# Two attention layers on one core: the output projection by the twice-applied seven-product scheme, in one row with k and q

## The chip, the cores and the metric

The kernel runs on one core of a Trainium2 chip. The metric is device time in microseconds, the median of several executions. A core has a matrix engine (TensorE, PE in the profile, with its weight loads as PEld), a vector engine (DVE), a scalar engine (ACT), a general engine (GpSimd, POOL) that is hardly used here, and a sync engine (SP) that issues all transfers of this kernel. Each takes its instructions in the order in which they were written; they wait for each other with semaphores. Products collect in PSUM, everything else on chip lies in SBUF, and weights and images come from and go to device memory (HBM).

## What is computed

Two attention layers follow each other on an input of 8 images with 512 channels and 32 x 32 = 1024 tokens, all in 32-bit floats. One layer is:

```
xn = group_norm(x) * gamma + beta            # 8 groups of 64 channels
q, k, v = Wq xn + bq, Wk xn + bk, Wv xn + bv # each 512 x 512 times 512 x 1024
e = exp(q^T k / 8)                           # 8 heads of 64 channels, 1024 x 1024 each
o = (e v) / (row sums of e)
x = x + Wp o + bp
```

## The kernel before

**Jobs.** An image in a layer is a job. The 16 jobs go in the order image 0 and 1 in layer 0, the same in layer 1, then images 2 and 3, and so on (`jobs`). Between the attention of job n and that of job n+1 lies a boundary; there are 15. At a boundary stand, on TensorE, the v product of job n+1 (`v_phase`), the output product of job n (`proj_phase`), and then k and q of job n+1 (`deep_phases`). After the last job a plain product stands instead (`plain_proj`).

**Seven products.** A product of two matrices cut into 2 x 2 blocks can be made with seven block products in place of eight, at the price of sums: some of blocks before (of weights, `factor`, kept in HBM by `store_factors`; of activations, `combine` and `inner_sums`), some of products after. `chain` does the sums after on four PSUM banks, named z, y, u and w by their use. Products 1, 6, 7 and 4 collect in z one after the other; between them z is copied (to y after 1, to u after 6) or read out (by `put(1, 1, z)` after 7 and `put(1, 0, z)` after 4). Product 3 collects in u. Product 4 can therefore not write z before `put(1, 1, z)` has read it. In `put` the results of the left half of the tokens go by the scalar engine, those of the right half by the vector engine. v and the output use the scheme once; both go in steps of half a block product, with the banks of one half of PSUM for each step in turn (`half_phase`). k and q use it twice: an outer scheme of seven products (order `OUTER`: 1, 2, 6, 5, 7, 3, 4), each of which is a chain of seven matmuls of 128 x 128 by 256 (order `ORDER`: 1, 5, 6, 2, 7, 3, 4). The chains overlap: position 7c + 2j orders product j of chain c. After products 7 and 3 of a chain one waiting addition of the outer scheme (`outer`) is issued, or an extra piece of work if there is none.

**Attention.** 64 steps per job (`Attention.run`): step i makes the scores of a block (four quarter matmuls of 512), their exponential on the scalar engine into one of five tiles e, the addition of that tile to `acc` on the vector engine (`add`), and the product of an earlier tile with v (`values`, two steps behind). Every eighth step ends a group (`finish`): DVE reduces `acc` to row sums r and joins the two halves of po into q's place (which then holds o); after every second group the sums r go through lr (by DMA), are inverted into rt (`invert`), written out to rd and read back as rb, repeated over 64 rows; `normalise` multiplies. Other work is put between the steps as `chores` with a step number: the group norm of the next job (`groups`, then `scale` and `shift`) and the sums of its blocks (`sums`).

**Order.** For TensorE, ACT and DVE the order is the order in which Python issues; a virtual clock (`advance`, `later`) decides when delayed pieces are issued, and knows nothing of an engine's load. Weights come through a ring of eight tiles (`fetch`, `plan`), a new one when an old one is used up. Tiles of one name take the same place: to with k, the block sums `deep` with raw weights that jobs 0 to 2 factor during attention, `acc`, `px` and `rb` with two places each, and x with two.

**Where the change touches.** `half_phase` from line 401, `v_phase`, `proj_phase` from line 455 (L469 the output products, L476 and L481 its results on DVE), `deep_phases` from line 492 (L538 the products, L552 and L554 results on DVE, L570 the outer additions), `combine` (L332 to L338), `inner_sums` (L370 to L376), `out_sums`, `deep_sums`, `make_out_bias`, and the main loop. Unchanged, but spoken of: L659 scores, L664 exponentials, L674 and L676 additions to `acc`, L690 values, L703 and L710 the end of a group, L724 to L730 the inversion, L740 the normalisation.

Of the kernel before, what the change touches and what calls it, by code (L numbers as in the profile page):

```python
# [70 lines left out]
def fast_path(  # L71
# [21 lines left out]
    out_bias = acts.tile([P, 2, NC], F32, name="out_bias")  # L93
    bias_step = acts.tile([P, 2, 2, 2], F32, name="bias_step")
# [71 lines left out]
    def fetch():  # L166


        if not plan or len(held) == RING:
            return  # L170
        key = plan.popleft()
        n, which, o = key
        layer = jobs[n][1]
        w = ring.tile([P, NW, P], F32, tag="w", name=f"w_{which}_{n}_{o}")
        held[key] = w
        if which in (V, O):
            nc.sync.dma_start(wide(w), factors[which, layer][:, FACTOR[o]])
        elif (which, layer, o) in deep:
            nc.sync.dma_start(w, deep[which, layer, o])
        else:  # L180
            if o in BLOCK:
                src = raw_block(layer, which, *BLOCK[o])
            else:
                src = factors[which, layer][:, FACTOR[o]]
            nc.sync.dma_start(wide(w), src)
            raw.add(key)
# [214 lines left out]
    def half_phase(n, which, src, t, group, order):  # L401

        steps = []
        for i in range(2):
            z, y, u, w = (bank(i, b, f"{b}_{which}_{n}_{i}") for b in "zyuv")
            steps.append(chain(*group(i), z, y, u, w))
        thunks = []
        for o in order:
            key = (n, which, o)
            thunks.append(lambda o=o: (steps[0](o), advance(1.72)))  # L410

            def second(o=o, key=key):
                steps[1](o)
                if key in held:
                    used(key)
                advance(1.72)

            thunks.append(second)
        return thunks

    def v_phase(n, order, first=None):
# [31 lines left out]
        return half_phase(n, V, src, tx, group, order)  # L453

    def proj_phase(n):
        b, layer = jobs[n]
        xt, src = xs[b], qt[0]

        def group(i):
            s5 = epool.tile([P, 2, HALF], F32, tag="e", name=f"s5o_{n}_{i}")  # L460

            def at(oh, sh):
                return xt[:, 2 * oh + i, sh * HALF : (sh + 1) * HALF]

            def product(o, ps, start):
                w = wide(held[n, O, o])
                r = right(src, to[0], o)
                for cc in range(2):
                    nc.tensor.matmul(  # L469
                        ps, w[:, cc, i * P : (i + 1) * P], r[:, cc, :],  # L470
                        start=(start and cc == 0), stop=(cc == 1), skip_group_check=True,
                    )

            def put5(ps):
                for oh in range(2):
                    nc.vector.tensor_add(s5[:, oh, :], ps, at(oh, 1))  # L476

            def put(oh, sh, ps):
                oc = 2 * oh + i
                more = s5[:, oh, :] if sh == 1 else at(oh, 0)  # L480
                nc.vector.scalar_tensor_tensor(  # L481
                    at(oh, sh), ps, out_bias[:, layer, oc : oc + 1], more, ALU.add, ALU.add
                )
                if layer == 1:
                    cols = slice(sh * HALF, (sh + 1) * HALF)
                    nc.sync.dma_start(out[b, oc * P : (oc + 1) * P, cols], at(oh, sh))

            return product, put5, put

        return half_phase(n, O, src, to, group, ORDER)  # L490

    def deep_phases(n, extra=()):
# [3 lines left out]
        extra = deque(extra)  # L496
        layer = jobs[n][1]
        dst = {}
        chains = [(K, o) for o in OUTER] + [(Q, o) for o in OUTER]
        tiles = {}  # L500

        def begin(c):
            which, o = chains[c]
            if o == OUTER[0]:
# [3 lines left out]
            if c + 2 < len(chains):  # L508
                prepare((n,) + chains[c + 2])
# [3 lines left out]
            half = c % 2  # L513
# [3 lines left out]
            r = right(xn[0], tx[0], o)  # L517
            if o in (4, 5, 6):
                sums = deep_t[0][:, :, {5: 0, 6: 1, 4: 2}[o], :]
            else:  # L520
                at = {1: 0, 7: 1, 2: 2, 3: 3}[o]
                sums = deep_x[0][:, :, at, :]
            moving = {
                1: r[:, 0, :QT], 2: r[:, 1, :QT], 3: r[:, 1, QT:],
                5: sums[:, 0, :], 6: sums[:, 1, :], 7: sums[:, 2, :], 4: sums[:, 3, :],
            }
            lhs = held[n, which, o]

            def bias(oo):
                if o in (1, 6, 7):  # L530
                    return None
                if o == 3:
                    return bias_step[:, layer, int(which == Q), oo : oo + 1]
                oc = oo if o == 2 else 2 + oo
# [23 lines left out]
        def end(c):  # L558
            which, o = chains[c]
            used((n, which, o))  # L560
            d = dst[which]

            def quarter(oh, sh):
                return d[:, 2 * oh : 2 * oh + 2, sh * HALF : (sh + 1) * HALF]
# [4 lines left out]
            def add(to_, a, b):  # L569
                outer.append(lambda: nc.vector.tensor_add(to_, a, b))  # L570

# [15 lines left out]
        outer = deque()  # L587

        def thunk(c, j):
            def go():  # L590
# [3 lines left out]
                if ORDER[j] in (7, 3):  # L594
                    if outer:
# [3 lines left out]
                if j == 6:  # L599
                    end(c)  # L600
                    if c + 1 == len(chains):
                        while outer:
                            outer.popleft()()
                        while extra:
                            extra.popleft()[1]()
# [3 lines left out]

        at = sorted((7 * c + 2 * j, c, j) for c in range(len(chains)) for j in range(7))  # L610
# [173 lines left out]
    def out_sums(n, src):  # L784
        def start():
            to[0] = acts.tile([P, 3, 2, HALF], F32, tag="k", name=f"to_{n}")
            combine(src, to[0], 0)

        later(12.6, start)
        for part in range(1, 4):  # L790
            later(12.6 + part * 1.7, lambda part=part: combine(src, to[0], part))

    def deep_sums(n, direct_at, other_at):


        def start():
            d = acts.tile([P, 4, 7, QT], F32, tag="deep", name=f"deep_{n}")
            deep_x[0], deep_t[0] = d[:, :, :4, :], d[:, :, 4:, :]

        later(direct_at - 0.1, start)  # L800
        for part in range(4):
            later(direct_at + 1.7 * part, lambda part=part: inner_sums(part, True))
            later(other_at + 1.7 * part, lambda part=part: inner_sums(part, False))
# [6 lines left out]
    def make_out_bias(layer, delay):  # L810
# [3 lines left out]
            apool.tile([P, 2, HALF], F32, tag="acc", name=f"rows_{layer}_{i}") for i in range(2)  # L814
# [8 lines left out]
        def part(oc):  # L823
# [3 lines left out]
            if oc == NC - 1:  # L827
# [3 lines left out]
                )  # L831

# [3 lines left out]
    def first_factors(chores, which_layers):  # L836
# [8 lines left out]
        chores[3] = start  # L845
        at = 14
        for i, (which, layer) in enumerate(which_layers):
            for part in range(4):
                at += 4
                chores[at] = lambda i=i, part=part: factor(box[0][:, i], part)  # L850
            chores[at + 1] = lambda i=i, which=which, layer=layer: store_factors(
                box[0][:, i], layer, which
            )
# [105 lines left out]
    deep_sums(0, 0.2, 12.0)  # L959
# [5 lines left out]
    rest = first[-1:]  # L965
    for n in range(-1, len(jobs)):
        last = n + 1 == len(jobs)
        if n >= 0:
            chores = {}
            if last:  # L970
                w = plain_weights(n)
            else:
                t = sums(n + 1)
                chores = dict(zip(range(2, 18), reads)) if n == 0 else {}
                chores.update(zip((24, 36, 40, 44, 48, 52), steps))
                chores.update({56: t[0], 60: t[1]})
                more = {}
                if n == 0:
                    first_factors(more, [(O, 0), (V, 1)])
                elif n == 1:  # L980
                    first_factors(more, [(K, 1), (Q, 1)])
                elif n == 2:
                    first_factors(more, [(O, 1)])
                for i, fn in more.items():
                    while i in chores:
                        i += 1
                    chores[i] = fn
                chores[61] = lambda: (extend_plan(n + 1), [fetch() for _ in range(RING)])
# [9 lines left out]
            t[2]()  # L998
            t[3]()
            out_sums(n, qt[0])  # L1000
            deep_sums(n + 1, 4.0, 27.0)
            if n in (0, 2):
                make_out_bias(jobs[n][1], 19.0)
            for thunk in v_phase(n + 1, ORDER):
                thunk()
            proj = proj_phase(n)
            for thunk in proj[:-1]:
                thunk()
            rest = proj[-1:]
        reads = steps = []  # L1010
        if n + 2 < len(jobs):
            reads, steps = norm_steps(n + 2)
        if n < 0:
            extra = [(0, lambda part=part: factor(q0, part)) for part in range(4)]
            extra.append((1, lambda: store_factors(q0, 0, Q)))
        else:
            extra, reads = [(7, fn) for fn in reads], []
        both = deep_phases(n + 1, extra)
        prepare((n + 1, K, OUTER[0]))
        prepare((n + 1, K, OUTER[1]))  # L1020
        both[0]()
        rest[0]()
        if n >= 0 and jobs[n][1] == 1 and jobs[n][0] + 2 < B:
            x_tile(jobs[n][0] + 2)
            load_x(jobs[n][0] + 2)
# [4 lines left out]
        att_n = n + 1  # L1030
        banks(0, "two")
        att = Attention(att_n)
# [254 lines left out]
```

## Time and profile before

| | |
|---|---|
| median of 3 executions | 3257.69 us (3254.89 to 3257.72) |
| the profiled execution | 3255.77 us, its span 3254.0 us |
| PE busy | 3238.2 us |
| DVE busy | 2569.5 us |
| ACT busy | 1729.5 us |
| from one job's first v product to the next job's | 201.57 us for most jobs, 203.08 once |
| additions L674 and L676 | 896, 1.22 us each |
| output: matmuls of 512 columns (L469) | 840 records in pairs |
| block sums for k and q (L370 to L376) | 64 of 1024 (1.21 to 1.23 us) and 64 of 768 (0.95 us) |

A line of the profile's groups names a source line, engine, operation, what is written and read, shape and count; then busy time and mean duration in ns; then the idle time of the engine ahead of it and what ended it. A line of the timeline has the start from the beginning of the span, the duration, the engine and line, and in square brackets the idle time ahead of it. In windows, each row is a stretch of time with its length, then the busy time of each engine. A matmul of 32-bit floats stands as two records.

### The profile page before, as it was taken

The numbers are of one execution on the slowest core, as the hardware profiler recorded it, in microseconds if no ns is written. First come the engines' busy times: TensorE is split into PE (matmuls) and PEld (weight loads), VectorE is DVE, ScalarE is ACT, GpSimd is POOL, SyncE is SP. The second block draws the span as 40 slices with busy tenths as digits, with TensorE's granted clock in tenths as the row PEclk, the third lists the DMA queues.
The fourth block names the chain that finished last, engine by engine and source line by source line (L and its number), as shares of the span: only waits on it lengthen the run. The fifth ranks groups of instructions, "written<-read, shape, count | busy, mean of one in ns | idle before, by whom it ended". The sixth has DMA issues, their size and how long they took to land.

```text
span 3254.0 us, 55636 instructions
## 1 busy us (share of the span) xinstructions
PE 3238.2 (100%) x22240; PEld 1730.1 (53%) x22240; DVE 2569.5 (79%) x3371; ACT 1729.5 (53%) x2561; POOL 14.4 (0%) x31
## 2 busy tenths in 40 slices
PE   9999999999999999999999999999999999999999
PEld 7356473564735547355463654636556364563643
DVE  8987978879687796868968689686886868868676
ACT  4636636366463664636546365463654636546363
POOL 0000000000000000000000000000000000000000
PEclk9999999999999999999999999999999999999999
DMA  8233251320502213032150311304114031130401
GB/s 299 73 112 93 71 167 57 112 96 26 176 19 79 66 32 116 15 114 85 35 164 16 93 54 38 109 16 148 51 42 157 18 105 40 48 99 22 132 21 49
DMA packets 149082, 265.53 MB, mean 82 GB/s; under 512 B 47832, under 2 KB 59216, under 8 KB 147792
## 3 DMA queue, kind: packets, MB, share of 16 engines
q1 hardware_dynamic: 148816, 261.91, 25.9%
q8 instruction: 176, 2.88, 0.4%
q14 instruction: 90, 0.74, 0.1%
HBM read 214.84 MB, written 44.89 MB: 80 GB/s over the span
## 4 chain that ended last, share of the span: by engine, by line
PE 97%; DVE 2%; DMA 0%; issue 0%; ACT 0%; SPq 0%; POOL 0%; DVEq 0%
PE sc L659 27%; PE po L690 27%; PE vd L538 8%; PE zd L538 7%; PE z L434 7%; PE z L469 6%; PE yd L538 3%; PE ud L538 3%; PE u L434 2%; PE v L434 2%; PE y L434 2%; PE y L469 2%; PE u L469 2%; PE v L469 2%; PE pp L628 1%; DVE p L554 0%
## 5 line engine op out<-in xcount | busy, mean ns | idle before, releaser
L664 ACT ACTIVATE e<-sc 128x1024 f32<-128x1024 f32 x1024 | 1046.6, 1024 | 585.7 <-PE sc L659 495.0
L659 PE MATMUL sc<-q,k 64*64 64x512 f32 x8192 | 1061.6, 590 | 0.0
L690 PE MATMUL po<-e,v 64*64 64x512 f32 x8192 | 1057.2, 589 | 0.0
L676 DVE TENSOR_TENSOR acc<-acc,e 128x1024 f32<-128x1024 f32 x768 | 938.1, 1222 | 72.7 <-ACT e L664 17.0
L690 PEld LDWEIGHTS po<-e,v 64*64 64x64 f32 x8192 | 312.9, 133 | 566.1 <-issue 551.9
L659 PEld LDWEIGHTS sc<-q,k 64*64 64x64 f32 x8192 | 309.9, 133 | 558.8 <-issue 546.1
L538 PE MATMUL vd<-deep,w 128*128 128x256 f32 x960 | 271.1, 383 | 4.5 <-DVE p L554 3.9
L674 DVE TENSOR_TENSOR acc<-e,e 128x1024 f32<-128x1024 f32 x128 | 155.9, 1218 | 108.9 <-ACT e L664 107.1
L538 PE MATMUL zd<-deep,w 128*128 128x256 f32 x832 | 232.8, 380 | 2.8 <-DVE p L552 2.0
L538 PEld LDWEIGHTS vd<-deep,w 128*128 128x128 f32 x960 | 179.4, 190 | 48.1 <-issue 13.0
L538 PEld LDWEIGHTS zd<-deep,w 128*128 128x128 f32 x832 | 157.7, 190 | 32.4 <-issue 6.9
L703 DVE TRANSPOSE_TENSOR_REDUCE r<-acc 128x32 f32<-128x1024 f32 x128 | 158.6, 1239 | 0.6
L385 ACT COPY yd<-vd 128x256 f32<-128x256 f32 x128 | 45.7, 357 | 185.1 <-PE vd L538 178.2
L740 DVE TENSOR_TENSOR q<-q,rb 128x512 f32<-128x512 f32 x128 | 83.3, 681 | 43.0 <-DMA rb<-rd 43.0
L469 PE MATMUL z<-to,w 128*128 128x512 f32 x240 | 110.3, 592 | 0.0
L434 PE MATMUL z<-w,xn 128*128 128x256 f32 x480 | 110.1, 382 | 0.0
L434 PE MATMUL z<-w,t 128*128 128x256 f32 x480 | 108.6, 379 | 0.0
L469 PE MATMUL z<-q,w 128*128 128x512 f32 x240 | 107.9, 592 | 0.0
L434 PEld LDWEIGHTS z<-w,xn 128*128 128x128 f32 x480 | 90.0, 190 | 23.8 <-issue 12.2
L389 ACT COPY u<-z 128x512 f32<-128x512 f32 x62 | 35.3, 570 | 121.8 <-PE z L469 85.1
L434 PEld LDWEIGHTS z<-w,t 128*128 128x128 f32 x480 | 91.0, 190 | 12.6 <-DVE v L449 0.2
L447 ACT COPY v<-z 128x512 f32<-128x512 f32 x32 | 18.8, 586 | 146.4 <-PE z L434 136.1
(172 smaller groups left out, 3385.2 us busy)
## 6 DMA issues: line engine op xcount, KB each, us to landing
w<-deep SPq DMA_DIRECT2D x196, 448.0 KB
w<-keep SPq DMA_DIRECT2D x226, 256.0 KB
rb<-rd SPq DMA_DIRECT2D x256, 128.0 KB
out_dram<-x SPq DMA_DIRECT2D x64, 256.0 KB
x<-x_dram SPq DMA_DIRECT2D x28, 512.0 KB
deep<-w SPq DMA_DIRECT2D x28, 448.0 KB
keep<-raw SPq DMA_DIRECT2D x5, 1792.0 KB
lr<-r SPq DMA_DIRECT2D x256, 8.0 KB
```

The lines of the kernel that those rows point to most:

```text
L385: nc.scalar.copy(y, z)
L389: nc.scalar.copy(u, z)
L434: nc.tensor.matmul(ps[:, ti * CH : (ti + 1) * CH], r[:, cc, t0 : t0 + P], w[:, cc, :], start=(start and ti == 0 and cc == 0), stop=(cc == ...
L469: nc.tensor.matmul(ps, w[:, cc, i * P : (i + 1) * P], r[:, cc, :], start=(start and cc == 0), stop=(cc == 1), skip_group_check=True,)
L538: nc.tensor.matmul(ps, lhs[:, FACTOR[i], :], moving[i], start=start, stop=True, skip_group_check=True,)
L659: nc.tensor.matmul(sc[h * HD : (h + 1) * HD, j, :], k[r, hp, k0 : k0 + HD], q[r, hp, sh * HALF : (sh + 1) * HALF], start=True, stop=True,)
L664: nc.scalar.activation(e, sc, AF.Exp, scale=SCALE)
L674: nc.vector.tensor_add(acc[g], self.es[i - 1], e)
L676: nc.vector.tensor_add(acc[g], acc[g], e)
L690: nc.tensor.matmul(po[g][j * HD : (j + 1) * HD, h, :], v[r, kc, d0 : d0 + HD], e[r, j, :], start=(kc == 0), stop=(kc == NT - 1),)
L703: nc.vector.tensor_reduce(self.r[:, m, :], self.acc.pop(g).rearrange("p j (b e) -> p (j b) e", e=RP), AX.X, ALU.add, apply_transpose=True,)
L740: nc.vector.tensor_mul(place[i], place[i], rb[i])
```

## The change

The output product also becomes a double scheme. Its seven outer products are the first seven chains of a row of 21, with k and q behind them; `proj_phase` is gone. Each O chain needs its activations as block sums of a quarter: `OutputSums` makes them on DVE, four of 128 x 256 per chain, those of five chains in v's phase (`out_sums`) and those of the last two in the row, as `soon`. The results of a chain go to a tile p with the bias (`out_bias`, and `out_step` for outer product 3), and 11 additions of 128 x 1024 bring the p tiles into x. A finished quarter of x is written out as one transfer of 512 KB (two of 256 KB before). Weights of O are factored a second time at their first use and then kept in HBM as those of k and q are, 448 KB per outer product in place of 256.

Moved with it: the group norm of the next job stands at earlier steps of attention, all four sums for v stand in attention (two of them stood after it), and from job 3 on the eight block sums for k and q stand in attention steps 46 to 60 (they stood in v's phase and the output). In jobs 0 to 2 three of these stay near the start of v's phase and five fall at the start of the row. The bias row products move from the output's phase into v's, the load of the next x to the second chain of k, and the statistics of the next norm to q's chains, with what is left over in the next attention. The last half steps of v change places, and the row of 21 begins in the other half of PSUM.

```diff
-    def proj_phase(n):
...
+    def sums_of_four(r, slots):
+        def blk(a, b):
+            return r[:, a, b * QT : (b + 1) * QT]
+        def first():
+            nc.vector.tensor_sub(slots[0], blk(0, 1), blk(0, 0))
+            nc.vector.tensor_sub(slots[1], blk(1, 1), slots[0])
+        def second():
+            nc.vector.tensor_sub(slots[2], blk(1, 1), blk(0, 1))
+            nc.vector.tensor_sub(slots[3], blk(1, 0), slots[1])
+        return first, second
...
+    def deep_phases(n, extra, outs=None):
...
-        chains = [(K, o) for o in OUTER] + [(Q, o) for o in OUTER]
+        chains = [(which, o) for which in ((O, K, Q) if outs else (K, Q)) for o in OUTER]
...
+            if which == O and c in (3, 4):
+                soon.extend(outs.steps(c + 2))
...
-            half = c % 2
+            half = (c + len(chains)) % 2
...
+            if which == O:
+                r = right(outs.src, to[0], o)
+                sums = outs.at[c]
...
+            if which == O:
+                b, layer = jobs[m]
+                xt = xs[b]
+                def more(oh, sh, *parts):
+                    to_ = xt[:, 2 * oh : 2 * oh + 2, sh * HALF : (sh + 1) * HALF]
+                    for part in parts:
+                        add(to_, to_, p(part))
...
+                if o == 1:
+                    more(0, 0, 1)
+                elif o == 2:
+                    more(0, 0, 2)
+                    done(0, 0)
+                elif o == 6:
+                    add(p(6), p(6), p(1))
+                    more(0, 1, 6)
+                elif o == 5:
+                    more(0, 1, 5)
+                elif o == 7:
+                    add(p(7), p(7), p(6))
+                    more(1, 1, 7, 5)
+                    done(1, 1)
+                elif o == 3:
+                    more(1, 0, 7)
+                    more(0, 1, 3)
+                    done(0, 1)
+                elif o == 4:
+                    more(1, 0, 4)
+                    done(1, 0)
+                return
...
                 if ORDER[j] in (7, 3):
+                    if soon:
+                        soon.popleft()()
                     if outer:
                         outer.popleft()()
...
-    def out_sums(n, src):
+    def out_sums(n, outs):
...
+        steps = outs.steps(0) + [start] + outs.steps(1) + [part(1)] + outs.steps(2)
+        steps += outs.steps(3) + [part(2)] + outs.steps(4) + [part(3)]
+        for i, step in enumerate(steps):
+            later((10.4 if i < 2 else 11.6) + 0.8 * i, step)
...
-                t = sums(n + 1)
-                chores = dict(zip(range(2, 18), reads)) if n == 0 else {}
-                chores.update(zip((24, 36, 40, 44, 48, 52), steps))
-                chores.update({56: t[0], 60: t[1]})
...
+                for i, fn in enumerate(reads if n == 0 else [fn for _, fn in extra]):
+                    put(2 + i, fn)
+                for i, fn in zip((18, 26, 28, 30, 32, 34, 37, 40, 42, 44), steps + sums(n + 1)):
+                    put(i, fn)
+                if n > 2:
+                    for i, fn in enumerate(deep_steps(n + 1)):
+                        put(46 + 2 * i, fn)
...
-            t[2]()
-            t[3]()
-            out_sums(n, qt[0])
-            deep_sums(n + 1, 4.0, 27.0)
+            outs = OutputSums(n)
+            out_sums(n, outs)
             if n in (0, 2):
-                make_out_bias(jobs[n][1], 19.0)
-            for thunk in v_phase(n + 1, ORDER):
-                thunk()
-            proj = proj_phase(n)
-            for thunk in proj[:-1]:
-                thunk()
-            rest = proj[-1:]
+                later(0.5, lambda layer=jobs[n][1]: make_out_bias(layer, 3.5))
+            if n <= 2:
+                for i, step in enumerate(deep_steps(n + 1)):
+                    later((1.0 if i < 3 else 20.0) + 1.5 * i, step)
+            first = v_phase(n + 1, ORDER)
+            for thunk in first[:-1]:
+                thunk()
+            rest = first[-1:]
```

## The prediction

> **What bounds the kernel now.** I read the page's busy shares and chain first, then the chain in order of time, then the busy time by stage of one late period (job 10 to job 11, then job 11's attention), last the vector engine's (DVE's) timeline at one stage boundary.
>
> ```profile
> PE 3238.2 (100%) x22240; PEld 1730.1 (53%) x22240; DVE 2569.5 (79%) x3371; ACT 1729.5 (53%) x2561; POOL 14.4 (0%) x31
> PE 97%; DVE 2%; DMA 0%; issue 0%; ACT 0%; SPq 0%; POOL 0%; DVEq 0%
> ```
>
> ```profile
> 418.69 3.45 PE z L434 x16
> 422.14 3.43 PE z L469 x8
> ...
> 1003.99 3.65 PE z L434 x16
> ```
>
> TensorE never rests, so its work is the time. In the chain by time, each of V's seven products (line 434) is eight matmuls of 256 columns, two records each, in 3.45 us: 0.431 us a matmul. Each output product (line 469) is four of 512 columns in 3.43 us, 0.858 each.
>
> ```profile
> 2213.40:2237.60 24.20, 24.20 (x116) 21.33 (x113) 20.73 (x26) 5.80 (x10) 0.00 (x0) 1.00 0.33 89
> 2237.60:2261.70 24.10, 24.10 (x59) 10.87 (x59) 10.35 (x14) 3.22 (x6) 0.00 (x0) 1.00 0.62 187
> 2261.70:2303.80 42.10, 42.10 (x202) 36.17 (x204) 29.24 (x48) 26.15 (x68) 0.00 (x0) 1.00 0.54 184
> 2303.80:2415.00 111.20, 110.99 (x1027) 39.53 (x1019) 97.33 (x114) 72.93 (x76) 0.53 (x1) 1.00 0.08 21
> ```
>
> The rows are V, output, k and q, attention; after the length come PE, PEld, DVE, ACT busy. DVE has 14 us to spare in attention of 111, and 14 in the output stage of 24: it is second everywhere, and close.
>
> ```profile
> 1005.15 1.25 DVE L703 TRANSPOSE_TENSOR_REDUCE r<-acc 128x32 f32<-128x1024 f32 x1
> 1006.32 0.65 DVE L710 TENSOR_TENSOR q<-po,px 128x512 f32<-128x512 f32 x1
> ...
> 1010.13 0.59 DVE L724 TENSOR_REDUCE lt<-lr 32x64 f32<-32x256 f32 x1 [0.90 <-DMA lr<-r]
> 1010.75 0.54 DVE L725 RECIPROCAL ri<-lt 32x64 f32<-32x64 f32 x1
> 1011.33 0.29 DVE L727 STREAM_TRANSPOSE rt<-ri 32x32 f32<-32x32 f32 x2
> ...
> 1016.76 0.69 DVE L740 TENSOR_TENSOR q<-q,rb 128x512 f32<-128x512 f32 x1 [1.37 <-DMA rb<-rd]
> 1018.77 0.69 DVE L740 TENSOR_TENSOR q<-q,rb 128x512 f32<-128x512 f32 x1 [1.31 <-DMA rb<-rd]
> ...
> 1061.07 0.42 DVE L552 TENSOR_TENSOR p<-zd,s 128x256 f32<-128x256 f32 x1 [1.67 <-PE zd L538]
> 1061.41 1.22 DVE L570 TENSOR_TENSOR k<-p,p 128x1024 f32<-128x1024 f32 x1
> 1062.54 0.42 DVE L552 TENSOR_TENSOR p<-ud,s 128x256 f32<-128x256 f32 x1
> ```
>
> V of this boundary (job 4 to job 5) starts at T0 = 1003.99, the chain's last line above. The last heads' sums leave DVE at T0+2.4, return through lr 3.7 us later, go out through rd and rb, and q is complete only at T0+15.4. Starts also show what an instruction occupies: 1.13 us for 1024 elements, 0.60 for 512, 0.34 for 256 (0.40 with a bias), about 0.13 more where it reads what the instruction just ahead wrote (three accumulating adds take 3.78).
>
> [...]
>
> **The change part by part.** TensorE, output: 28 matmuls x 0.858 = 24.0 us become 49 x 0.431 = 21.1. Gain 2.9 us at each of 15 boundaries, 44 in all. The scalar engine gets the same per-chain copies as in k and q (26 us in 42) and stays hidden.
>
> DVE, output: four sums of two and eight results (4 x 0.60 + 8 x 0.66 = 7.7 us) go; 14 results of 256 (5.2), 11 adds of 1024 (12.4) and 28 block sums of 256 (about 10.2) come: 20 us more per boundary. Two sums of xn move from V into attention, and from job 3 on (12 boundaries) all eight block sums for k and q too: 4 x 1.13 + 4 x 0.87 = 8.0 us.
>
> *Attention, jobs 3 to 14.* A running sum over DVE's instructions in the order of the changed program, from the add of e37, which starts 43.9 us ahead of T0: 24 adds 27.1, nine dependent gaps 1.2, four reductions 4.6, four q<-po 2.4, four normalisations 2.4, one inversion 1.9, four sums of xn 4.5, eight block sums 8.0. That is 52.1 us of work in 43.9, so q<-po ends at T0+8.3. The same sum over the order of before gives T0+2.6 where the trace has T0+3.0, so T0+8.6: DVE is 5.6 us later than now. The adds then run up to 7.8 us behind their exponentials. Five e tiles cover that all but 0.6 us, so attention itself still looks full.
>
> *V, same jobs.* V's second half needs the last po banks: its second product should start there at T0+5.2 and waits until T0+8.7. The sums now leave at T0+8.0, lr lands at 11.75, rt is ready at 13.25, rb lands 5.1 and 7.1 us after it, normalisation ends at T0+21.0. Only then come the five sets of block sums (4 x 0.34 + 0.13 = 1.5 each, 7.5), four sums of 1024 (4.5) and V's four results (2.4), with a few gaps: 14.8 us, to T0+35.8. Queued behind them is the first DVE result of the row, which must empty z before the seventh product of the same chain writes it. Undisturbed, that product starts at T0+28.0 (V's thirteenth half step at T0+20.7, then two half steps of 1.72 and nine matmuls). Now it starts at T0+36.2. Stall: 8.2 us, the 3.5 in V included.
>
> *The row, same jobs.* A chain lasts 3.0 us. DVE per chain, from the second: 1.9, 3.3, 4.6 (two adds, two results, four block sums), 1.8, then three of 3.06. Two heavy chains put 1.9 us in excess against some 0.7 of slack between a result and the product that waits for it: about 1.1 us more. With some 0.2 for rb sharing the DMA engines with a 448 KB weight load (256 before), 9.5 us of stall. Net 9.5 - 2.9 = +6.6, times 12 = +79 us.
>
> *Jobs 0 to 2.* The block sums for k and q stay in V and the row: three fit ahead of the inversion, five (4.6 us) fall on the row's first chains. Jobs 0 and 2 also factor the output weights (seven sets of four sums, about 1.0 us a set) and make the output bias (four parts of 1.33 us about the normalisation), on the same queue. Job 0: by the running sum q<-po ends at T0+4.6; normalisation, behind three bias parts, at 17.2; the last part and V's list of 14.8 at 33.6; four factor sets and two block sums at 39.7; first result 40.0 against 28.0, so 12.0, and 4.5 more in the next four chains, which carry the remaining sums: 16.5. Job 2, whose q<-po is 1.9 earlier: 14.5. Job 1 (no bias, output weights kept): normalisation 16.9, list 31.7, two block sums, result at 34.0: 6.0, and 5.4 where k's weights are factored, of which 1.5 is in this period already: 9.9. Together 40.9; less 2.9 each, +32 us.
>
> *Weights and SP.* O weights grow by 192 KB, 20 MB in all over 15 boundaries. SP is held by rd and rb until T0+17, then issues five loads: 2.2 MB at the 230 GB/s of T0+12 to T0+16 is 9.7 us, while the third is needed after T0+33. Hidden; were one late, each us costs 12. The x load moves from the start of k to its second chain, over 18 us ahead of its first reading: nothing. Output transfers are as many bytes, hidden under k.
>
> Sum: -44 + 12 x 9.5 + 40.9 = +111, on the profiled execution's 3255.8 us (span 3254.0): 3367. The median shown is 1.9 above that execution: 3369, say 3370.
>
> Unknowns, from both sides: a block sum on SBUF alone is not in the trace; 0.30 to 0.42 each, taken 0.34 from the PSUM row, gives -1 to +2 us over the 20 in V. rb under load, 0 to 1.5 us. DVE's lateness, 4.6 to 6.6. Per boundary 7.5 to 12.
>
> **Rivals.** *TensorE alone decides* (faster): all of DVE's work fits in its gaps, 44 us come in, 3214. It needs DVE through V's list by about T0+28; the trace gives rb's landing at T0+14.8 even with no lateness, and 14.8 us of list behind it end at T0+30.2, already 2 us over. It decides only if the late sums are cheaper than their rows by half and attention adds no lateness. 7 in 100. *Lateness half absorbed*: the wait in V and the one in the row are the same wait seen twice, or lr and rb come back faster after an idle stretch; stall 4.5 to 6, jobs 3 to 14 cost +19 to +37, 3310 to 3330. 12 in 100. *DVE bound throughout*: each chain of 3.06 against 3.0 also drags, and the e tiles stall attention beyond 0.6: 2 to 3 us more a boundary, 3395 to 3415. 12 in 100. *No net change*: stall near 2.9 at all boundaries; 2 in 100.
>
> **How the numbers follow.** The reckoned case, 3340 to 3395, has 67 in 100 and sets 3370. The range 3310 to 3405 leaves out the fast cases below and the end of the DVE-bound one above. About 0.2% (6.5 us) is what a measurement of this kernel tells from no change: faster 0.07, same 0.02, slower 0.91.
>
> **What would show it.** PE busy below 97% of the span; PE waits on DVE of some 150 us in all against 7 now. The longest at the row's first chain (on DVE's result) and at V's second product in the second half (on q<-po), both at every boundary from job 3. q<-po about 8 us after V's first product instead of 3. DVE without idle through the last 27 attention steps. V to V: 208 us for jobs 3 to 14 against 201.6. It is wrong if DVE rests before the row's first result, or if the adds in attention trail by less than 4 us.

## The result, and the profile after

The changed kernel took 3437.6 us (median of 4, 3433.3 to 3440.0) against 3256.4 us: a ratio of 1.0555, with a 95% interval of 1.0537 to 1.0573. Slower was right; 3370 was not, nor does the range hold the time. The profiled execution took 3439.2 us, its span is 3437.4.

The page's busy shares, and its chain that ended last:

```profile
PE 3263.7 (95%) x22870; PEld 1855.9 (54%) x22870; DVE 2858.0 (83%) x4044; ACT 1894.5 (55%) x3026; POOL 24.0 (1%) x31
PE 49%; DVE 31%; DMA 8%; issue 7%; SPq 3%; ACT 2%; POOL 0%; DVEq 0%; ACTq 0%; POOLq 0%
```

TensorE rests 174 us, and the chain runs half outside it, where it was 97% TensorE. Line numbers below are those of the changed kernel where nothing else is said: L733 scores, L738 exponentials, L764 values, L748 and L750 additions to `acc`, L784 the end of a group (q<-po), L439 V's products and L454 their results on DVE, L567 the row's products and L581 and L583 their results on DVE, L258 mr, L269 scaling, L275 shift, L802 rd, L808 rb, L814 the normalisation. What TensorE waited for (us in total, times, longest):

```profile
PE sc L733 <- ACT e L738: 47.6, 16, 6.6
PE vd L567 <- DVE p L581: 39.3, 31, 3.8
PE v L439 <- DVE q L784: 27.2, 12, 2.3
PE z L439 <- DVE v L454: 20.1, 12, 2.7
...
PE po L764 <- ACT e L738: 7.3, 12, 1.1
```

The second, third and fourth lines are the boundary, at the places that the prediction named (the row's first results, q<-po, V's results). The first and the last are attention, waiting for exponentials: 55 us that the prediction did not have.

The busy time by stage of one period, job 10 to job 11 and then job 11's attention (length, then PE, PEld, DVE, ACT and POOL busy, granted clock, DMA share, GB/s):

```profile
2351.60:2378.40 26.80, 23.11 (x108) 19.70 (x105) 17.50 (x29) 5.21 (x9) 0.00 (x0) 1.00 0.37 124
2378.40:2446.10 67.70, 64.85 (x301) 55.85 (x299) 55.49 (x95) 40.48 (x106) 0.00 (x0) 1.00 0.55 181
2446.10:2561.40 115.30, 112.39 (x1031) 39.63 (x1031) 102.86 (x120) 73.32 (x77) 1.41 (x1) 1.00 0.08 22
```

The rows are V, the row of 21 and attention. The first two replace 89.4 us of V, output, k and q (V to first scores), the third 112.2. Summed over the whole trace, by where V, the row and the scores start:

| | before | after | difference | predicted |
|---|---|---|---|---|
| V and row, boundaries of jobs 0 to 2 | 269.8 | 301.9 | +32.1 | +32 |
| V and row, jobs 3 to 14 | 1072.9 | 1143.0 | +70.1 | +79 (12 x (9.5 - 2.9)) |
| attention of jobs 0 to 14 | 1682.5 | 1762.0 | +79.5 | 0 |

The 9.5 us of stall in the prediction's sum are 8.2, 1.1 and an estimated 0.2, all at the boundary; the 0.6 us that it names for attention is in none of the terms, so its sum has nothing there. The boundaries came out 9 us under what was reckoned (102 against 111), and the miss of some 70 us lies in attention, which the prediction took to stay full. Jobs 4 to 14 take 115.3 to 117.6 us there, jobs 0 to 3 117.5 to 121.9, against 112.2 before. The 1.7 us that are left of the difference stand ahead of the first attention.

**Where attention stops.** The timeline of job 13's attention after the change:

```profile
2907.95 1.32 SPq L258 DMA_DIRECT2D mr<-dg  x2
...
2909.36 0.56 SPq L802 DMA_DIRECT2D rd<-rt  x1
...
2914.94 3.15 SPq L808 DMA_DIRECT2D rb<-rd  x4
...
2919.13 0.69 DVE L814 TENSOR_TENSOR q<-q,rb 128x512 f32<-128x512 f32 x1 [2.17 <-DMA rb<-rd]
2920.66 0.69 DVE L814 TENSOR_TENSOR q<-q,rb 128x512 f32<-128x512 f32 x1 [0.84 <-DMA rb<-rd]
...
2922.60 0.81 DVE L269 TENSOR_SCALAR xn<-x,mr,mul 128x1024 f32<-128x1024 f32 x1
...
2923.45 1.15 ACT L275 ACTIVATE xn<-xn,vec_sb 128x1024 f32<-128x1024 f32 x1 [4.33 <-DVE xn L269]
...
2925.56 1.99 PE L733 MATMUL sc<-q,k 64*64 64x512 f32 x8 [3.24 <-ACT e L738]
```

And the same pair of heads in the kernel before:

```profile
2746.41 0.33 SPq L728 DMA_DIRECT2D rd<-rt  x1
...
2747.79 2.41 SPq L734 DMA_DIRECT2D rb<-rd  x4
...
2753.12 1.28 SPq L257 DMA_DIRECT2D mr<-dg  x2
```

Before, the norm's small transfers (mr) come after rd and rb; rb is issued 1.38 us after rd. After, `groups` stands at step 18 in place of 24, so that mr is issued just ahead of rd: rb, which waits for rd to land, is issued 5.58 us after it. It is so each time: in the changed kernel rb follows rd by 4.7 to 5.6 us in the 15 pairs with mr just ahead, and by 1.4 to 2.5 in the 49 others. What went over the DMA queues in the 4.3 us from the issue of rd:

```profile
DMA packets 455, 0.00 MB, mean 1 GB/s; under 512 B 455, under 2 KB 455, under 8 KB 455
```

mr is only 4 KB, but 512 packets of 8 bytes. In the packet records they run from 1.4 to 6.2 us after the issue of mr. The 64 packets of rd, on the same queue, as a rule run 0.8 to 1.0 us after their issue where no mr is ahead; in all 15 pairs with mr their last one comes at the end of mr's packets, within 0.1 us. So rd waits behind the packets of mr, though mr has only half as many bytes.

DVE stands still for the late rb, so the scaling behind it is late; the shift, now two steps behind the scaling, waits 4.33 us on ACT; the exponentials queue behind the shift; TensorE stops for 3.24 us. The last line shows something more: eight records take 1.99 us where they take 1.04 elsewhere. The granted clock in the same place (length, PE busy, clock, DMA share, GB/s):

```profile
2923.00:2924.00 1.00, 0.00 (x0) 1.00 0.00 0
2924.00:2925.00 1.00, 0.00 (x0) 0.96 0.00 0
2925.00:2926.00 1.00, 0.44 (x4) 0.50 0.00 0
2926.00:2927.00 1.00, 1.00 (x8) 0.50 0.00 0
2927.00:2928.00 1.00, 1.00 (x8) 0.50 0.00 0
2928.00:2929.00 1.00, 1.00 (x12) 0.84 0.00 0
```

After the stop TensorE runs at half clock for 3.41 us and loses 1.71. Up to the end of its work the trace has 23 such stretches, four of them double, which lose 46 us in all, against none before: 22 us of it in attention, 22 at the boundaries, the rest at the start. So attention's 79.5 us are 55 of stops, 22 of lost clock, and some 2.4 not accounted for.

### The profile page after: what moved, and what is told of

Read it like the earlier page. It is cut to its first block, busy times and chain, and to the rows that moved or that the text cites. A ratio compares the mean times of both kernels' runs of the same rounds, so it can differ in the third digit from the quotient of the medians.

```text
span 3437.4 us, 58046 instructions
## 1 busy us (share of the span) xinstructions
PE 3263.7 (95%) x22870; PEld 1855.9 (54%) x22870; DVE 2858.0 (83%) x4044; ACT 1894.5 (55%) x3026; POOL 24.0 (1%) x31
## 4 chain that ended last, share of the span: by engine, by line
PE 49%; DVE 31%; DMA 8%; issue 7%; SPq 3%; ACT 2%; POOL 0%; DVEq 0%; ACTq 0%; POOLq 0%
PE sc L733 13%; PE po L764 11%; DVE acc L750 10%; PE vd L567 9%; PE zd L567 8%; PE yd L567 3%; DMA rd<-rt 3%; PE ud L567 3%; DMA rb<-rd 3%; DVE acc L748 2%; DMA lr<-r 2%; ACT e L738 1%; SPq L808 1%; DVE x L596 1%; SPq L790 1%
## 5 line engine op out<-in xcount | busy, mean ns | idle before, releaser
L738 ACT ACTIVATE e<-sc 128x1024 f32<-128x1024 f32 x1024 | 1043.7, 1023 | 602.8 <-PE sc L733 483.1
L733 PE MATMUL sc<-q,k 64*64 64x512 f32 x8192 | 1071.9, 596 | 49.6 <-ACT e L738 47.6
L764 PE MATMUL po<-e,v 64*64 64x512 f32 x8192 | 1066.9, 594 | 7.3 <-ACT e L738 7.3
L750 DVE TENSOR_TENSOR acc<-acc,e 128x1024 f32<-128x1024 f32 x768 | 936.1, 1219 | 57.5 <-ACT e L738 17.5
L733 PEld LDWEIGHTS sc<-q,k 64*64 64x64 f32 x8192 | 307.9, 134 | 623.5 <-issue 537.1
L764 PEld LDWEIGHTS po<-e,v 64*64 64x64 f32 x8192 | 311.2, 134 | 587.7 <-issue 559.0
L567 PE MATMUL vd<-deep,w 128*128 128x256 f32 x900 | 256.5, 384 | 5.6 <-DVE p L583 5.1
L567 PE MATMUL zd<-deep,w 128*128 128x256 f32 x892 | 248.2, 380 | 3.4 <-DVE p L581 3.2
L748 DVE TENSOR_TENSOR acc<-e,e 128x1024 f32<-128x1024 f32 x128 | 156.4, 1222 | 103.1 <-ACT e L738 102.9
L567 PEld LDWEIGHTS vd<-deep,w 128*128 128x128 f32 x900 | 168.2, 190 | 48.6 <-DVE p L583 13.1
L814 DVE TENSOR_TENSOR q<-q,rb 128x512 f32<-128x512 f32 x128 | 84.9, 684 | 122.9 <-DMA rb<-rd 122.9
L567 PEld LDWEIGHTS zd<-deep,w 128*128 128x128 f32 x892 | 169.4, 190 | 27.9 <-DVE p L581 4.0
L567 PE MATMUL vd<-os,w 128*128 128x256 f32 x420 | 128.9, 395 | 39.0 <-DVE p L581 38.8
L596 DVE TENSOR_TENSOR x<-x,p 128x1024 f32<-128x1024 f32 x135 | 164.4, 1218 | 0.1
L439 PE MATMUL z<-w,t 128*128 128x256 f32 x480 | 118.6, 397 | 20.2 <-DVE v L454 20.1
L439 PEld LDWEIGHTS z<-w,t 128*128 128x128 f32 x480 | 95.3, 201 | 40.2 <-DVE v L454 26.0
L596 DVE TENSOR_TENSOR p<-p,p 128x1024 f32<-128x1024 f32 x94 | 114.3, 1216 | 0.0
L275 ACT ACTIVATE xn<-xn,vec_sb 128x1024 f32<-128x1024 f32 (+1 forms) x68 | 74.0, 1097 | 73.0 <-DVE xn L269 73.0
L567 PEld LDWEIGHTS vd<-os,w 128*128 128x128 f32 x420 | 77.3, 192 | 64.8 <-DVE p L581 50.9
L585 ACT COPY s<-zd 128x256 f32<-128x256 f32 x173 | 64.7, 374 | 85.9 <-PE zd L567 85.9
```

Of the source, the lines that this page charges most:

```text
L275: nc.scalar.activation(xn[0][:, cc, cols], xn[0][:, cc, cols], AF.Identity, bias=env.vec(self.layer, BETA, cc),)
L439: nc.tensor.matmul(ps[:, ti * CH : (ti + 1) * CH], r[:, cc, t0 : t0 + P], w[:, cc, :], start=(start and ti == 0 and cc == 0), stop=(cc == ...
L567: nc.tensor.matmul(ps, lhs[:, FACTOR[i], :], moving[i], start=start, stop=True, skip_group_check=True,)
L585: return chain(product, lambda ps: nc.scalar.copy(s5, ps), put, z, y, u, w)
L733: nc.tensor.matmul(sc[h * HD : (h + 1) * HD, j, :], k[r, hp, k0 : k0 + HD], q[r, hp, sh * HALF : (sh + 1) * HALF], start=True, stop=True,)
L738: nc.scalar.activation(e, sc, AF.Exp, scale=SCALE)
```

## The experiments

**Theory A**: attention's loss comes from the norm's work that was moved, by the two steps just read. Rivals: only one of them counts (S, Q), or the load of block sums on DVE is the cause (L).

**Transfers of the norm earlier.**

```diff
-for i, fn in zip((18, 26, 28, 30, 32, 34, 37, ...), steps + sums(n + 1)):
+for i, fn in zip((18 if n == 0 else 9, 26, 28, 30, 32, 34, 37, ...), steps + sums(n + 1)):
```

> The changed kernel with one thing undone: the small transfers of the group norm (dg, mr) stand at attention step 9 in place of 18, clear of the pair of rd and rb that normalises the heads just ahead of the scaling. Theory A (these transfers delay rd and rb, the normalisation waits on the vector engine, the scaling and with it the shift come late, the scalar engine cannot make exponentials, TensorE stops): most of the attention's extra time goes, 113 to 114 us from attention to V instead of 116.5 for jobs 4 to 14; about 3 us and half of the slow-clock stretches in attention for each of 14 jobs, 3365 to 3395 us. Rival S (only the shift's distance of two steps behind its scaling matters): no more than 15 us less, 3420 to 3440. Rival L (the vector engine's load of adds and block sums in attention is the cause): no change, 3430 to 3445.

3391.1 us, 46.5 less; ratio to before 1.0409 (1.0391 to 1.0426). Jobs 4 to 14 took 113.4 to 114.1 us in attention; job 0, where the transfers stay at step 18, took 120.7, about as in the changed kernel (120.5). rb follows rd by at most 2.2 us in all pairs but the one of job 0. Rivals S and L fall as the only cause. The waits for exponentials went from 55 to 21 us.

**Shifts later.**

```diff
-for cc in range(NC + 1):
+for cc in range(NC + 2):
...
-if cc > 0:
-    shift(cc - 1)
+if cc > 1:
+    shift(cc - 2)
```

The step list gets one place more for this, 36, and the first of the four sums of xn stands at 38 in place of 37.

> The changed kernel with one thing changed: a shift on the scalar engine stands two scalings (four steps) behind its own scaling instead of one (two steps). The late rb stays. Theory A says the late scaling only hurts because the shift waits in the scalar engine's order ahead of the exponentials; with 3.4 us more the first shift no longer waits: 3360 to 3400 us, and the waits of the scalar engine for the scaling fall from 73 us to under 30. Rival Q (the vector engine itself, held up by the late rb, delays the adds until the five e tiles are used up): little changes, over 3420. Rival L (load): no change, 3430 to 3445.

3418.9 us, 18.7 less; ratio 1.0498 (1.0481 to 1.0516). ACT's waits for the scaling fell from 73 to 15 us as expected, but the time missed my 3360 to 3400 and lies just under rival Q's bound. DVE still waits 124 us for rb (123 in the changed kernel), and TensorE still 40 us for exponentials, in stops of at most 2.0 us. So the late rb does harm through DVE too, not only through the shift.

**Both.** The two edits together:

> The changed kernel with both: the group norm's transfers at step 9 and the shifts four steps behind their scalings. Theory A: TensorE's waits for exponentials (55 us now) all but vanish and the attention of jobs 4 to 14 takes 112.4 to 113 us; 3355 to 3380 us, what is left over the time before being the boundary alone. Rival L: 3425 to 3445.

3374.9 us, 62.7 less; ratio 1.0365 (1.0347 to 1.0382). The two edits nearly add up (65.2). TensorE's waits now:

```profile
PE vd L567 <- DVE p L581: 37.2, 30, 3.8
PE z L439 <- DVE v L454: 30.1, 14, 4.0
PE v L439 <- DVE q L784: 27.2, 12, 2.3
PE po L764 <- ACT e L738: 9.2, 12, 1.1
...
PE sc L733 <- ACT e L738: 2.2, 3, 1.6
```

Attention takes 112.2 to 113.5 us (job 0 115.2), the boundaries are as in the changed kernel (103.5 us over before in all, against 102.2). With attention repaired the time is near the predicted 3370; what that is worth is said below.

**One part alone, on the kernel before.**

```diff
-chores.update(zip((24, 36, 40, 44, 48, 52), steps))
+chores.update(zip((18, 26, 28, 30, 32, 34), steps))
```

> The kernel before with one part of the change alone: the group norm's work at attention steps 18 (groups), 26, 28, 30, 32, 34 (scalings and shifts) in place of 24, 36, 40, 44, 48, 52. No block sums are added and the output product is untouched. Theory A: the attention slows by this alone, by 3 to 6 us for each of 15 jobs with the slow-clock stretches after the stops, 3300 to 3345 us. Rival L (it takes the block sums' load as well): within 10 us of before, 3250 to 3267 us.

3315.3 us; ratio 1.0176 (1.0159 to 1.0193). The move alone costs 58 us, with no block sum added. The timeline of one of its attentions:

```profile
1373.70 0.81 DVE L268 TENSOR_SCALAR xn<-x,mr,mul 128x1024 f32<-128x1024 f32 x1
...
1374.55 1.15 ACT L274 ACTIVATE xn<-xn,vec_sb 128x1024 f32<-128x1024 f32 x1 [4.34 <-DVE xn L268]
...
1376.66 1.99 PE L659 MATMUL sc<-q,k 64*64 64x512 f32 x8 [3.25 <-ACT e L664]
```

It is the same chain as in the changed kernel (4.33 and 3.24 there); the lengths differ from job to job, with stops of 2.1 to 4.1 us here and 1.9 to 6.6 there. Attention of jobs 0 to 14 is 62.7 us over before in this run, 43.5 of it in stops and 17 in lost clock, and with both repairs 14.9 us are left of the changed kernel's 79.5. The two, 77.6, nearly make up the whole: theory A holds from both sides, and for the load of rival L there is no more than some 15 us.

**The boundary: block sums for k and q left out**, on the version with both repairs. Theory B is that the boundary stops because DVE comes out of attention late.

```diff
-if n > 2:
+if n == 3:
     for i, fn in enumerate(deep_steps(n + 1)):
```

> Built on the version with both attention repairs (norm transfers early, shifts later). The eight block sums for k and q are left out from job 5's on: that job and the later ones multiply with the sums made for job 4, so this part of the computation is missing in 11 of the 15 boundaries, 8.0 us of the vector engine's time in each attention. Theory B (the boundary stops because the vector engine leaves attention late, and its list in V ends late by the same amount): V's stop of 2.3 us on q<-po goes and so do the waits on V's results and on the row's first result; about 6 us and some slow-clock stretches for each of 11 boundaries, 3300 to 3325 us against 3375. Rival V (the list of block sums behind rb's return sets the end whatever the lateness): only the 2.3 us go, 3340 to 3355.

The time, 9685 us, answers nothing: with the old sums in use the kernel's own limit on the softmax sums is passed, and it computes everything again on its general path. The first 3300 us of the trace are the run that was meant. There, V and row take 88.6 to 90.7 us for the boundaries without the sums, against 95.2 in the version with both repairs, and a period 202.0 against 208.3: 6.3 less, where theory B gave about 6. TensorE's waits over one such period:

```profile
PE vd L567 <- DVE p L581: 2.7, 2, 1.8
PE vd L567 <- DVE p L583: 0.2, 1, 0.2
```

and over a period with both repairs and the sums:

```profile
PE vd L567 <- DVE p L581: 2.7, 2, 1.8
PE v L439 <- DVE q L784: 2.3, 1, 2.3
PE z L439 <- DVE v L454: 1.9, 1, 1.9
PE po L764 <- ACT e L738: 0.7, 1, 0.7
PE vd L567 <- DVE p L583: 0.2, 1, 0.2
```

Both of V's stops and attention's 0.7 go with DVE's lateness, and so at all 11 boundaries without the sums; the row's own 2.7 (1.0 to 2.7 over the 11) stay, against theory B, which had the first of them go too. So even with 8.0 us of DVE's work gone, V and row take 89.9 us, and 89.4 in the kernel before.

**Part of the output's sums left out.**

```diff
-sums = outs.at[c]
+sums = outs.at[2 if c in (3, 4) else c]
...
-steps += outs.steps(3) + [part(2)] + outs.steps(4) + [part(3)]
+steps += [part(2), part(3)]
```

> Built on the version with both attention repairs. In V's list two of the five sets of block sums of the output (chains 3 and 4) are left out, and these chains use the sums of chain 2: eight subtractions of 128 x 256, about 3.0 us, are missing from the computation at each of 15 boundaries. The lateness out of attention stays. Theory B and rival V both expect the waits behind the list (V's results, row's first result, 3 to 4 us) to shrink by up to 3 us, while the 2.3 us on q<-po stay: 3325 to 3345. If the list does not matter (only the weights' or rb's transfers do): over 3360.

3354.6 us; ratio 1.0304 (1.0287 to 1.0321): less than expected. Boundaries of jobs 0 to 2 gained 3.5 us each, those of jobs 3 to 14 only 1.1. The waits on the row's results fell from 37.2 to 20.3 us. Of V's two stops the one on q<-po stayed (27.2 and 27.6) and the one on V's results fell only from 30.1 to 21.9; the sets that are left out stand in DVE's list behind the result that V waits for. Waits for copies on ACT (7.5 us) came in. At the boundaries of jobs 3 to 14 TensorE rests 17.5 us less, but 6.9 us more are lost to the clock (15.4 against 8.5), which takes part of the gain back.

**Spread.**

```diff
-zip((18 if n == 0 else 9, 26, 28, 30, 32, 34, 36, 38, 40, 42, 44), ...)
+zip((18, 26, 28, ...) if n == 0 else (9, 14, 16, 18, 20, 22, 24, 26, 29, 32, 35), ...)
...
-put(46 + 2 * i, fn)
+put(38 + 2 * i, fn)
```

> Built on the version with both attention repairs. All work is there; from job 1 on the scalings stand at attention steps 14 to 20, the sums of xn at 24 to 35 and the block sums for k and q at 38 to 52 in place of 46 to 60, so that the vector engine has ten steps without them at the end. Theory B: the lateness of 5.6 us at the end shrinks by what the last steps leave free, some 3 to 5 us; V's 2.3 us stop and part of the row's go: 3320 to 3350. Rival F (the vector engine is full in all of the attention, 108 of 111 us, so the lateness only moves and the e tiles run out earlier): 3365 to 3400.

3371.4 us; ratio 1.0349 (1.0332 to 1.0366). Theory B's 3320 to 3350 was wrong, rival F right: V's wait on q<-po fell from 27.2 to 11.0 us, but the waits for exponentials rose from 11.4 to 15.3 us, and attention from 113.1 to 113.7. The boundaries of jobs 3 to 14 gained 15.8 us in all, attention lost 9.3: for the most part the lateness only moved.

**GpSimd makes the block sums for k and q.** In `inner_sums`, four times:

```diff
-nc.vector.tensor_sub(...)
+nc.gpsimd.tensor_sub(...)
```

> Built on the version with both attention repairs. All work is there; the eight block sums for k and q are made by GpSimd, which is idle, in place of the vector engine, at all boundaries. Theory B, with the two engines independent: as with the sums left out, and jobs 0 to 2 gain too: 3285 to 3320. Rival G (GpSimd takes longer than the vector engine [...]): the additions to acc become longer than 1.22 us, and the time stays at or over 3375.

3485.4 us; ratio 1.0700 (1.0682 to 1.0718): rival G. The timeline of one attention:

```profile
2780.64 3.34 POOL L375 TENSOR_TENSOR deep<-xn 128x1024 f32<-128x1024 f32 x1
2781.69 3.38 DVE L339 TENSOR_TENSOR t<-xn,t 128x1024 f32<-128x1024 f32 x1
2783.94 3.32 POOL L373 TENSOR_TENSOR deep<-xn,deep 128x1024 f32<-128x1024 f32 x1
2784.99 9.40 DVE L750 TENSOR_TENSOR acc<-acc,e 128x1024 f32<-128x1024 f32 x3
```

One sum takes 3.3 us on GpSimd, and DVE's additions beside it about 3.1 each in place of 1.22. Over the run the 896 additions to acc take 1244.7 us, 152 more than with both repairs: 9.5 per attention, more than the 8.0 taken off. In the same timeline an addition to acc just ahead of GpSimd's first sum takes 1.21, and the reduction to r beside one of the sums 1.23, as in the kernel before (1.24): the additions grow beside the sums, this reduction doesn't. What makes them grow is not shown.

**Scaling off DVE**, on the spread version: xn in one activation, with a bias of beta minus mean times factor.

```diff
+nc.vector.tensor_mul(self.nb, self.mr[:, :, 0], self.mul)
+nc.vector.tensor_sub(self.nb, env.vec_sb[:, b0 : b0 + NC], self.nb)
...
-norm.scale(cc)
...
+nc.scalar.activation(xn[0][:, cc, :], xs[norm.b][:, cc, :], AF.Identity,
+    bias=norm.nb[:, cc : cc + 1], scale=norm.mul[:, cc : cc + 1])
```

> Built on the spread version (norm early, sums of xn at 24 to 35, block sums at 38 to 52). The scaling of the group norm leaves the vector engine: the scalar engine makes xn from x in one activation with scale and bias (it made one for the shift before), and the vector engine makes only two products of 128 x 4 for the bias. Nothing is left out. Theory B (the vector engine's time in attention is what a boundary waits for): 4 x 0.81 less 0.3, some 2.9 us less in each attention; the waits for exponentials (15 us in all) go and the lists in V end 2 to 3 us earlier at 12 boundaries, 3320 to 3345 us against 3371. Rival V (the list in V and the transfers of lr, rd and rb set the end by themselves): 3355 to 3370.

3342.3 us; ratio 1.0269 (1.0252 to 1.0286), the best of the variants and still behind the kernel before. The total is in theory B's range, the split is not: attention is back at 112.2 to 112.7 us, but V and row of jobs 3 to 14 fell only from 93.9 to 93.6 (3.0 us in all, where attention fell by 22), and the wait on q<-po is 11.0 as it was. That much of rival V is right.

**Stops by themselves**, in the kernel before.

```diff
-nc.scalar.activation(e, sc, AF.Exp, scale=SCALE)
+again = {10: 1 + n % 5, 30: 2 + n % 3, 58: 2 + (n + 1) % 4}.get(i, 0)
+for _ in range(1 + again):
+    nc.scalar.activation(e, sc, AF.Exp, scale=SCALE)
```

> The kernel before; at three places of each attention the exponential of one step is made one to five times more, 1.0 us each, so that TensorE stops for about 0.5 to 4 us. Nothing else is changed and the output is the same. Theory H (a stop of TensorE costs more than its length: where it is long enough, a stretch of 3.42 us at half clock follows, 1.71 us): no stretch after stops under 1.9 us, one after about half of the stops of 2 to 4 us, and the attention of each job is longer than 112.2 us by its stops and 1.71 for each stretch. Rival (the clock in the records has no part in the time): the attention is longer by its stops alone. In all some 80 to 110 us of stops and 20 to 40 us of lost clock: 3350 to 3405 us.

One execution, 3380.7 us. Each attention is 112.2 us, its stops, and its lost clock: job 4's 123.0 are 112.2 + 7.4 + 3.4 (123.0), job 12's 117.1 are 112.2 + 4.2 + 0 (116.4). The rival, stops alone, would give 119.6 for the first. Over the 15 attentions 0.0 to 0.7 us are left over with the lost clock counted, and 0.5 to 4.1 without it. Where no clock is lost, the rest is 0.23 us for each stop (0.47 with two, 0.69 with three). Of twelve stops of 1.7 to 1.8 us none was followed by half clock, of twelve of 2.7 to 2.9 seven, of seven of 3.9 six. Theory H holds in the time; what decides which stop is followed by a stretch stands in the last section.

## Why the prediction was wrong

- **TensorE's gain, 2.9 us a boundary**: too large. In the windows from job 10 to job 11, PE is busy 23.11 + 64.85 = 87.96 us where before took 89.4: 1.4. Over jobs 3 to 14, stops of 6.2 and lost clock of 1.3 a boundary make 7.4, and the boundary grew by 5.8, which leaves 1.6. Part of the missing 1.3 may be the stops again: at 0.23 us for each beside its length, as in the run with stops by themselves, the three or four stops of a boundary make 0.7 to 0.9, as an estimate. The rest isn't separated.
- **Attention still full but for 0.6 us**: this is the step that failed. The sum has nothing for attention, and it grew by 79.5 us; moving the norm's work alone made it grow by 62.7. The running sum of DVE's work was not at fault: with both repairs attention is at 113.1, 0.9 over, near the 0.6 reckoned. (Its 0.13 us for a dependent addition is a misreading: in the trace before, additions to `acc` in a row start 1.33 us apart and an independent instruction 1.14 after one, so 0.19. Over nine gaps that is 0.5 us.) What failed is what I didn't reckon. I gave the norm's new place no cost: not what the packets of its transfers do to rd on the queue, not what stands behind a late rb on DVE, nor what a shift two steps behind its scaling holds up on ACT.
- **V, jobs 3 to 14**: right in mechanism and place. In job 10 to job 11, V starts at T0 = 2351.6:

```profile
2358.64 0.65 DVE L784 TENSOR_TENSOR q<-po,px 128x512 f32<-128x512 f32 x1
...
2359.35 1.99 PE L439 MATMUL v<-w,t 128*128 128x256 f32 x8 [2.27 <-DVE q L784]
...
2370.56 0.69 DVE L814 TENSOR_TENSOR q<-q,rb 128x512 f32<-128x512 f32 x1 [0.54 <-DMA rb<-rd]
...
2376.57 1.99 PE L439 MATMUL z<-w,t 128*128 128x256 f32 x8 [1.42 <-DVE v L454]
...
2386.15 0.70 PE L567 MATMUL vd<-os,w 128*128 128x256 f32 x2 [1.75 <-DVE p L581]
```

  These lines are the timeline of the changed kernel. q<-po ends at T0+7.7 (8.6 predicted), V's second product waits 2.27 (3.5), normalisation ends at T0+19.7 (21.0), the row's waiting product starts at T0+34.6 (36.2). One stop more stands in V itself: its results lie on DVE among the sets. DVE does not rest between the normalisation and the row's first result, as foretold; in the 44 us of attention ahead of T0 it rests once, for 0.46 us, and its last addition ends 6.9 us after its exponential (7.8 predicted).
- **The row, 1.1 us of its own**: with the sums left out the row still waits up to 2.7 us, more than twice that. Together the stops are 6.2 a boundary in place of 9.5; the half clock (1.3), which I had not reckoned, and the smaller gain (1.6) make up most of the difference. That +70 came near +79, and the kernel with both repairs near 3370, is therefore partly luck.
- **Jobs 0 to 2**: +32.1 measured, +32 predicted, but the sum hides its parts: 13.6, 7.0 and 11.6 were predicted for jobs 0, 1 and 2, and 11.6, 10.3 and 10.3 came. 6.8 of it are lost clock, and 10.8 are two waits of 5.4 for factored weights in the row. No experiment takes this part alone, so the match is luck in part and its causes are not shown.
- **What would show it**: PE under 97% (95) was right. Waits on DVE were 109 us, not 150; the 55 on ACT should have been the warning that a wait was missing. V to V is about 212 us, not 208; with both repairs it is 208.3.
- **Rivals**: none had the cause. *DVE bound throughout* had attention stalling, but by the load of adds, which the one-part run rules out.
- **The half clock**: the profile before has no stretch of it, and I gave it no price at any stop. By the counts below, a stop of 3.2 to 4.2 us costs 2.0 us of clock on average and a longer one 2.8; the two stops that the prediction had at each of 12 boundaries (3.5 in V, 4.7 at the row) would have brought some 58 us, as an estimate. The stops that came were shorter, and so was their price (1.3 us a boundary).

## What to carry to other kernels

A chore that is moved has a cost on each in-order queue that it passes: ask which transfer is issued behind its transfers, which instruction waits for that, and what stands behind this one. Count a transfer's packets and not only its bytes: here 4 KB in 512 packets took 4.8 us. Keep a consumer on an engine that feeds the bound further behind its producer than the producer's worst lateness. When TensorE is full, price a stop of over 2 us at its length and the lost clock (here 0.9 to 2.8 us on average, by the length of the stop), and look for an engine with room before adding work to one that is nearly full.

## What the runs showed of the hardware

- Half clock after a stop. Over eight of the profiles (the changed kernel, both repairs alone and together, the norm moved alone, stops, spread, scaling off DVE), a stretch of half clock followed 2 of 293 stops of 0.8 to 1.95 us, 65 of 125 of 1.95 to 3.2 us, 24 of 26 of 3.2 to 4.2 us, and all 12 over that. One stretch is 3.41 us and costs 1.71; with double ones a stop of these four kinds costs 0.01, 0.9, 2.0 and 2.8 us of clock on average. So gaps of 1.95 to 3.2 us were already enough half of the time (65 of 125).
- What decides between stops of one length. In each of these profiles all stretches start on one grid of 3.413 us. Take the cells of that grid at full clock, from 20 us on, and add up TensorE's rest inside each: of 2601 cells with under 1.8 us of rest none was followed by a stretch, of 27 with 1.8 to 2.05 us eight, of 95 with more all. In the profiles not used for this (the kernel before, part of the output's sums left out, GpSimd, and the first 3290 us of the one with the sums for k and q left out) it was none of 1243 under 1.8 us and all 42 over 2.0. So in these runs a stop of 2 to 4 us costs clock or not by where it falls on the grid.
- Two small transfers (mr, 4 KB in 512 packets of 8 bytes) issued 1.4 us ahead of an 8 KB one (rd) put its return off from 1.4 to 5.6 us; the packets of mr took 4.8 us from the first to the last, and those of rd were not through before.
- GpSimd took 3.2 to 3.3 us for a subtraction of 128 x 1024 in the timeline of one attention, with DVE at work beside it, and DVE's additions beside these sums took 3.1 in place of 1.22. No run here has GpSimd alone, so how much of its time is its own, and whether the engines wait for each other, is not shown.
